# A shared ring of four PSUM buffers in a second layer's first spreading, and one-hots unpacked one and a half ranges ahead

## The chip, the cores and the metric

The kernel runs on one core of a Trainium2 chip. Times are device microseconds of that core. The engines are PE (TensorE: matmuls, with PEld for its weight loads), DVE (VectorE), ACT (ScalarE), POOL (GpSimd) and SP (SyncE, which here only issues DMAs). Each has its own instruction queue and works through it in order; they wait for each other by semaphores. Lines are those of the kernel before.

## The reference

Two layers of a graph network over 32,768 nodes of 128 features and 524,288 edges. The part that the change touches is the second layer: three rounds in which each node is mixed with a softmax memory and with the sum of its neighbours' scaled rows.

```python
# layer 0: x = layernorm(x + L0(x)); L0 sums x[src] into dst, has an MLP, attention and batch norms
for _ in range(3):                                   # layer 1
    q = x @ Wq.T + bq
    retrieved = softmax(q @ keys.T) @ values         # 512 keys
    deg = zeros(n).at[col].add(1.0);  dinv = rsqrt(deg)
    agg = zeros_like(x).at[row].add((dinv[:, None] * x)[col])      # over all edges
    lap = x - dinv[:, None] * agg
    x = 0.5 * x + 0.5 * (retrieved - 0.2 * lap)
x = layernorm(x_in + layernorm(x))
```

## The kernel before

Nodes are taken in 64 blocks (NB) of 512, a block in 4 chunks (NCH) of 128; a chunk of 128 nodes is also called a range, of which there are 256 (NW).

**Summing over edges** is done in two halves. *Spreading*: for each range of source nodes a one-hot matrix of 128 x 1536 (12 groups of 128 slots) copies the rows to slots of the outgoing edges. A row is 384 wide, three bf16 parts of an fp32 row of 128 (`split_steps`, L1394). `spread` (L1465) makes one *unit*: two matmuls (L1470, 128x128 by 128x384) into one `exp` tile of two PSUM banks, and one eviction of 128x768 into the bf16 tile `y_o`, by ACT (L1480) or by DVE (L1478). A range has KS = 6 units, a block 24. After every third unit half a range's slots, 576 KB, are stored by SP (L1483). `y_o` has two buffers, a range each. *Collecting*: `Sums` fetches for each range of targets the slots and some single rows (L1488, and POOL's indirect DMAs, L1497), builds one-hots (L1508) and adds with matmuls (L1522).

**The one-hot of a range** is kept in DRAM packed: its 1536 columns are three thirds, and each third has one bit of every packed byte. `ask_pick` calls `known_pick` (L1415), which has SP load the packed 64 KB (`three`, L1417). `unpack` calls `unpacked` (L1420), which takes them apart on DVE with one `bitwise_and` (`pick`, L1424). Before, `three` has three buffers and `pick` two (the pool's default).

**The second layer** is `layer1_grid` (L2042 on). It begins with a spreading by itself: the loop at L2298 over blocks, in pools `l1p`. It reads the first layer's result transposed (`v_d`), and so each block has a front part, `first`, that runs seven blocks ahead of the spreading: load `vT` and `x0`, `scale` on ACT (L2072), `turn` on PE (four transposes, L2077) with the addition to `x0` on DVE (L2078), `moments` on DVE (L2086, L2087), and for four blocks together a square root (L2092, L2093), then `norm` on DVE (L2098). `prepare` multiplies by dinv (L2109) and splits a row in three on ACT and DVE (L1403 to L1407). `emit` lists the 24 units and calls `ask_pick` two ranges ahead and `unpack` one range ahead, after the third unit of a range. Every third unit is DVE's. PSUM has eight banks: three `exp` tiles of two banks and two `tr` tiles of one for the transposes.

Then come two *steps* (pools `l1w`): collecting for state t, the softmax memory, and the spreading for state t + 1 woven together (every fourth unit is DVE's, two `exp` tiles), and a last step that collects only. `emit` is the same function in all of them.

The lists carry keys (`(12, turn)`), and `placed` sorts them into one program order. The spreading loop and the two steps are not in a `manual_schedule` block: a planner at build time orders the instructions of each engine's queue by its own costs, with the program order as the priority and the tiles' buffers as conditions.

Of the kernel before, what the change touches and what calls it, by code (L numbers as in the profile page):

```python
# [9 lines left out]
F32 = mybir.dt.float32  # L10
I32 = mybir.dt.int32
# [7 lines left out]
PSUM = bass.MemoryType.PSUM  # L19

P = 128
D = 128
BLK = 512
NCH = BLK // P
# [886 lines left out]
def tile_gnn_resnorm(ctx: ExitStack, tc: tile.TileContext, a: dict, out: bass.AP):  # L911
# [433 lines left out]
    def rows_of(t, i):  # L1345

        return t.rearrange("(b c p) d -> b p c d", c=NCH, p=P)[i]

    def kept_of(t, i):

        return t.rearrange("(b p c) d -> b p (c d)", c=NCH, p=P)[i]

    def flat(t):
        return t.rearrange("p c d -> p (c d)")
# [7 lines left out]
    class Exchange:  # L1362
# [50 lines left out]
            return t  # L1413

        def known_pick(self, wp, w):  # L1415
            packed = wp.tile([P, P], I32, name="three", bufs=3)
            nc.sync.dma_start(packed, pick_d[w])  # L1417
            return packed

        def unpacked(self, wp, packed):  # L1420


            pick = wp.tile([P, 3, P], I32, name="pick")
            nc.vector.tensor_tensor(pick, packed[:, None, :].to_broadcast([P, 3, P]),  # L1424
                                    gc["bits"].unsqueeze(2).to_broadcast([P, 3, P]), OP.bitwise_and)
            return pick.rearrange("p k n -> p (k n)").bitcast(FP8)
# [615 lines left out]
    def layer1_grid(v_d, s3, c3):  # L2042

        exs = [Exchange("src", slots_d[t % 2], rows_d[t]) for t in range(T_STEPS)]
        with tc.tile_pool(name="l1g", bufs=1) as gp:
# [3 lines left out]
            asked, picked = {}, {}  # L2049

            def ask_pick(wp, w):
                if w < NW:
                    asked[w] = exs[0].known_pick(wp, w)

            def unpack(wp, w):
                if w in asked:
                    picked[w] = exs[0].unpacked(wp, asked.pop(w))

            def first(b, st, wp, p_tr, group):

                k = b % NCH

                def load():
                    st["v"] = wp.tile([P, BLK], F32, name="vT", bufs=3)
                    nc.sync.dma_start(st["v"], v_d[b])
                    st["x0"] = wp.tile([P, NCH, D], F32, name="x1", bufs=2 * NCH)
                    nc.sync.dma_start(st["x0"], rows_of(a["x"], b))

                def scale():
                    nc.scalar.activation(st["v"], st["v"], AF.Identity, bias=c3, scale=s3)  # L2072

                def turn():
                    ps = p_tr.tile([P, NCH, P], F32, name="tr")
                    for c in range(NCH):
                        nc.tensor.transpose(ps[:, c, :], st["v"][:, c * P:(c + 1) * P], ident)  # L2077
                    nc.vector.tensor_add(st["x0"], st["x0"], ps)  # L2078

                def moments():  # L2080
                    if k == 0:
                        group["mv"] = wp.tile([P, NCH, NCH, 2], F32, name="ln_mvs")
                    st["mv"] = group["mv"]
                    t = wp.tile([P, NCH, 6], F32, name="ln_st")
                    for c in range(NCH):
                        nc.vector.bn_stats(t[:, c, :], st["x0"][:, c, :])  # L2086
                        nc.vector.bn_aggr(st["mv"][:, k, c, :], t[:, c, :])  # L2087
                    if k == 0:
                        group["rs"] = wp.tile([P, NCH, NCH], F32, name="ln_rss")
                    st["rs"] = group["rs"]  # L2090
                    if k == NCH - 1:
                        nc.scalar.activation(st["rs"], st["mv"][:, :, :, 1], AF.Sqrt, bias=eps_c)  # L2092
                        nc.vector.reciprocal(st["rs"], st["rs"])  # L2093

                def norm():
                    st["x"] = wp.tile([P, NCH, D], F32, name="xn", bufs=5)
                    for c in range(NCH):
                        nc.vector.tensor_scalar(st["x"][:, c, :], st["x0"][:, c, :], st["mv"][:, k, c, 0:1],  # L2098
                                                st["rs"][:, k, c:c + 1], op0=OP.subtract, op1=OP.mult)
                    nc.sync.dma_start(kept_of(xs_d[0], b), flat(st["x"]))  # L2100
                return load, [(7, scale), (12, turn), (15, moments)], [(14, norm)]

            def prepare(t, b, st, wp):
# [12 lines left out]
            def emit(t, b, st, wp, p_e, share):  # L2116

                ex = exs[t]
                y = {}

                def spread(n):
                    c, m = divmod(n, KS)
                    i = b * NCH + c
                    if m == 0:
                        ask_pick(wp, i + 2)
                        if i not in picked:
                            unpack(wp, i)
                    ex.spread(wp, p_e, "exp", i, picked[i], st["r"][:, c, :], m, y, n % share == share - 1,
                              WEIGHTS[m // 2])
                    if m == 2:  # L2130
                        unpack(wp, i + 1)
                    if m == KS - 1:
                        del picked[i]

                return [(n, lambda n=n: spread(n)) for n in range(NCH * KS)]
# [55 lines left out]
            def placed(*lists):  # L2191

                return [f for _, f in sorted((x for one in lists for x in one), key=lambda x: x[0])]
# [12 lines left out]
            def first_states(t, wp, p_s, p_tr):  # L2206

                for b in range(3):
                    ask_state(t, b, wp, p_s, p_tr)
                run(f for _, f in mems[0]["front"] + mems[0]["back"] + mems[1]["front"])  # L2210
# [77 lines left out]
            def run(steps):  # L2288
                for f in steps:
                    f()  # L2290

            with tc.tile_pool(name="l1p", bufs=2) as wp, \
                    tc.tile_pool(name="l1p_exp", bufs=3, space=PSUM) as p_e, \
                    tc.tile_pool(name="l1p_tr", bufs=2, space=PSUM) as p_tr:
                sts, firsts, norms, group = {}, {}, {}, {}
                for w0 in range(2):
                    ask_pick(wp, w0)
                for n in range(-NCH - 3, NB):  # L2298
                    b = n + NCH + 3
                    if b < NB:  # L2300
                        sts[b] = {}
                        load, firsts[b], norms[b] = first(b, sts[b], wp, p_tr, group)
                        load()
                    lists = []
                    if n + NCH + 2 in firsts:
                        lists.append(firsts.pop(n + NCH + 2))
                    if n + 2 in norms:
                        lists.append(norms.pop(n + 2))
                    if 0 <= n + 1 < NB:
                        lists.append(prepare(0, n + 1, sts[n + 1], wp))  # L2310
                    if n >= 0:
                        lists.append(emit(0, n, sts[n], wp, p_e, 3))
                    run(placed(*lists))
                    sts.pop(n, None)

            with tc.tile_pool(name="l1w", bufs=2) as wp, \
                    tc.tile_pool(name="l1_seg", bufs=2, space=PSUM) as p_g, \
                    tc.tile_pool(name="l1_exp", bufs=2, space=PSUM) as p_e, \
                    tc.tile_pool(name="l1_s", bufs=1, space=PSUM) as p_s, \
                    tc.tile_pool(name="l1_tr", bufs=1, space=PSUM) as p_tr:  # L2320
                for t in range(T_STEPS - 1):
                    sums = Sums(exs[t], wp, p_g, gc["iota1"], 2)
                    sts = {}
                    first_states(t, wp, p_s, p_tr)
                    for w0 in range(2):
                        ask_pick(wp, w0)
                    for n in range(-2, NB):
                        lists = []
                        if n + 1 in sts:
                            lists.append(prepare(t + 1, n + 1, sts[n + 1], wp))  # L2330
                        if n >= 0:
                            lists.append(emit(t + 1, n, sts[n], wp, p_e, 4))
                        b = n + 2
                        two_b = placed(*lists, *ahead(b))
                        if b < NB:
                            sts[b] = {}
                            weave(two_b, consume(t, b, sts[b], sums, wp, p_s, p_tr))
                        else:
                            run(two_b)
                        sts.pop(n, None)  # L2340
            with tc.tile_pool(name="l1z", bufs=2) as wp, \
# [6 lines left out]
                with tc.manual_schedule():  # L2348
# [3 lines left out]
                    for b in range(NB + 2):  # L2352
# [11 lines left out]
                        if b < NB:  # L2364
                            st = {}
# [95 lines left out]
```

## Time and profile before

Three runs: 14064.68, 14081.59 and 14114.55 us, median 14081.59. The profiled execution took 14078.42 us, its span from the first to the last instruction is 14076.6. Stages, by the starts and ends of their matmuls and loads, with the busy share of each engine in them (from the busy time of each stretch):

| stage | from, us | length, us | PE | DVE | ACT | POOL | clock | DMA share |
|---|---|---|---|---|---|---|---|---|
| sorting of edges, attention | 0 | 2345 | 85% | 80% | 48% | 37% | 0.93 | 0.06 |
| layer 0 spreading | 2345 | 1176 | 70% | 91% | 79% | 1% | 0.94 | 0.92 |
| layer 0 collecting, attention | 3521 | 2191 | 79% | 76% | 23% | 57% | 0.91 | 0.78 |
| layer 0 feed-forward | 5712 | 276 | 88% | 57% | 49% | 0% | 0.93 | 0.56 |
| layer 1 first spreading | 5988 | 1289 | 63% | 70% | 69% | 0% | 0.84 | 0.83 |
| layer 1 step 1 | 7277 | 2403 | 89% | 60% | 58% | 58% | 0.97 | 0.94 |
| layer 1 step 2 | 9680 | 2345 | 89% | 60% | 57% | 58% | 0.97 | 0.95 |
| layer 1 last step | 12025 | 2052 | 79% | 64% | 30% | 62% | 0.90 | 0.69 |

Over the whole span PE is busy 81%, DVE 70%, ACT 49%, POOL 44%, and the DMA engines move 251 GB/s. "Clock" is the TensorE clock that the throttle granted, 1.00 being full speed; "DMA share" is the mean busy share of the core's 16 DMA engines. A busy share is read together with what ends an engine's idle time: a stage in which no engine and no DMA stands near full is bound by their waiting for each other.

### The profile page before, as it was taken

The numbers are of one execution on the slowest core, as the hardware profiler recorded it, in microseconds if no ns is written. First come the engines' busy times: TensorE is split into PE (matmuls) and PEld (weight loads), VectorE is DVE, ScalarE is ACT, GpSimd is POOL, SyncE is SP. The second block draws the span as 40 slices with busy tenths as digits, with TensorE's granted clock in tenths as the row PEclk, the third lists the DMA queues.
The fourth block names the chain that finished last, engine by engine and source line by source line (L and its number), as shares of the span: only waits on it lengthen the run. The fifth ranks groups of instructions, "written<-read, shape, count | busy, mean of one in ns | idle before, by whom it ended". The sixth has DMA issues, their size and how long they took to land.

```text
span 14076.6 us, 165746 instructions
## 1 busy us (share of the span) xinstructions
PE 11459.8 (81%) x57832; PEld 5663.9 (40%) x57832; DVE 9833.9 (70%) x16418; ACT 6929.2 (49%) x10523; POOL 6149.7 (44%) x5525
## 2 busy tenths in 40 slices
PE   7898898777688888866668999897999888787887
PEld 2233233333333333322235555454555444344444
DVE  7978876997677777676656666565666555566667
ACT  4454455878122222466655665555665555333333
POOL 0273263000555555000015666554665555566665
PEclk9899998999899999988889999999999999898999
DMA  1000003999777877588879999998999999766676
GB/s 41 11 17 16 11 17 118 336 333 357 235 248 255 257 254 249 202 303 300 302 284 353 366 362 353 342 341 301 361 359 344 341 338 324 248 239 236 237 248 220
DMA packets 1401348, 3538.76 MB, mean 251 GB/s; under 512 B 218802, under 2 KB 633682, under 8 KB 1399346
## 3 DMA queue, kind: packets, MB, share of 16 engines
q1 hardware_dynamic: 960496, 2818.23, 55.1%
q0 software_dynamic: 252608, 520.41, 12.2%
q10 hardware_dynamic: 187394, 189.42, 4.1%
q8 instruction: 457, 7.49, 0.2%
q14 instruction: 393, 3.22, 0.1%
HBM read 2075.09 MB, written 1452.25 MB: 251 GB/s over the span
## 4 chain that ended last, share of the span: by engine, by line
PE 36%; DVE 8%; issue 5%; ACT 4%; another core or an unknown queue 3%; DMA 1%; SPq 0%; ACTq 0%; POOL 0%; DVEq 0%; POOLq 0%
PE seg L1522 14%; PE exp L1470 10%; PE s L2157 4%; PE s L2169 3%; DVE y_o L1478 3%; PE tr L2163 2%; ACT y_o L1480 2%; PE s L2149 1%; DVE oh L1508 1%; DMA slots<-y_o 1%; PE tr L2181 1%; PE tr L2143 1%; DVE pick L1424 0%; ACT pr L1064 0%
## 5 line engine op out<-in xcount | busy, mean ns | idle before, releaser
L1497 POOL DMA_INDIRECT listed<-rows,other x5120 | 5137.8, 1003 | 5234.2 <-issue 3027.3
L1470 PE MATMUL exp<-rows,pick 128*128 128x384 bf16 x10752 | 2620.3, 350 | 1004.0 <-ACT y_o L1480 309.6
L1480 ACT ACTIVATE y_o<-exp 128x768 bf16<-128x768 f32 x3328 | 2579.1, 811 | 1234.9 <-PE exp L1470 741.6
L1522 PEld LDWEIGHTS <-oh 128*128 128x128 bf16 x19456 | 1962.2, 101 | 2151.7 <-issue 1142.1
L1522 PE MATMUL seg<-y_i,oh 128*128 128x384 bf16 x12288 | 2586.9, 336 | 1.8 <-issue 1.5
L1470 PEld LDWEIGHTS <-pick 128*128 128x128 fp8e4 x10752 | 1082.2, 103 | 2355.1 <-issue 1552.1
L1478 DVE TENSOR_SCALAR y_o<-exp 128x768 bf16<-128x768 f32 x1280 | 1218.8, 952 | 832.8 <-PE exp L1470 559.8
L1688 ACT ACTIVATE pT<-s 128x1024 f32<-128x1024 f32 x1024 | 1047.8, 1024 | 1243.2 <-PE s L1663 822.9
L1522 PE MATMUL seg<-listed,oh 128*128 128x384 bf16 (+1 forms) x5120 | 1238.9, 341 | 356.6 <-ACT degs L2004 176.9
L1668 DVE TENSOR_REDUCE mx<-s 128x2 f32<-128x1024 f32 x1024 | 1244.7, 1219 | 314.7 <-PE s L1663 269.5
L1684 PE MATMUL s<-ql,k 32*128 32x512 f32 x4096 | 1222.1, 675 | 157.8 <-DVE mx L1668 145.1
L2233 DVE SCALAR_TENSOR_TENSOR part<-seg,dinv,part 128x128 f32<-128x128 f32 x1536 | 530.4, 345 | 1164.4 <-PE seg L1522 636.9
L1663 PE MATMUL s<-k,q 32*128 32x512 f32 x4096 | 1222.3, 677 | 15.8 <-ACT pT L1688 10.7
L1476 ACT CAST y_o<-exp 128x768 bf16<-128x768 f32 x1152 | 857.5, 809 | 241.8 <-PE exp L1470 172.1
L2157 PE MATMUL s<-keysT,qT 128*128 128x512 f32 x1536 | 830.3, 624 | 17.3 <-ACT qT L2151 6.3
L2163 PE MATMUL tr<-ident,pr 128*128 128x128 f32 x3072 | 536.4, 290 | 287.0 <-issue 216.7
L2169 PE MATMUL s<-pt,values 128*128 128x512 f32 x1536 | 722.5, 607 | 23.0 <-issue 20.1
L1508 DVE TENSOR_TENSOR oh<-iota,slot 128x2432 bf16<-128x2432 bf16 x512 | 724.6, 1415 | 7.5 <-PE tr L2163 4.2
L1062 DVE TENSOR_REDUCE nm<-s 128x1 f32<-128x512 f32 x768 | 517.8, 682 | 302.1 <-PE s L2157 106.8
L1508 DVE TENSOR_TENSOR oh<-ramp_p,slot 128x2432 bf16<-128x2432 bf16 x512 | 722.1, 1411 | 3.3 <-DMA slots<-y_o 3.2
L2164 ACT COPY pt<-tr 128x512 f32<-128x512 f32 x768 | 450.7, 588 | 469.6 <-remote 149.8
L1064 ACT ACTIVATE pr<-s,nm 128x512 f32<-128x512 f32 x768 | 528.8, 689 | 309.4 <-DVE nm L1062 187.5
(415 smaller groups left out, 15024.5 us busy)
## 6 DMA issues: line engine op xcount, KB each, us to landing
slots<-y_o SPq DMA_DIRECT2D x2048, 576.0 KB
y_i<-slots SPq DMA_DIRECT2D x1024, 1152.0 KB
listed<-rows,other POOLq DMA_INDIRECT x5120
rows<-rows SPq DMA_DIRECT2D x192, 384.0 KB
band<-row_dst SPq DMA_DIRECT2D x128, 384.0 KB
band<-row_src ACTq DMA_DIRECT2D x256, 192.0 KB
three<-pick SPq DMA_DIRECT2D x768, 64.0 KB
x_d<-xn SPq DMA_DIRECT2D x128, 256.0 KB
```

Of the source, the lines that this page charges most:

```text
L1470: nc.tensor.matmul(ps[:, j, :ROW], pick[:, o:o + P], r, start=True, stop=True)
L1478: nc.vector.tensor_scalar(dst, ps[:, :, :ROW], weight, None, op0=OP.mult)
L1480: nc.scalar.mul(dst, ps[:, :, :ROW], weight)
L1497: nc.gpsimd.indirect_dma_start(out=g[:, k, :], out_offset=None, in_=self.table, in_offset=bass.IndirectOffsetOnAxis(ap=index[:, k:k + 1], ...
L1508: nc.vector.tensor_tensor(oh.rearrange("p c (w z) -> p c w z", z=2), ramp.rearrange("p (w z) -> p w z", z=2)[:, None].to_broadcast([P, NC2 ...
L1522: nc.tensor.matmul(ps[:, :n], oh[:, j, :], src, start=(k == 0), stop=(k == NC2 - 1))
L1663: nc.tensor.matmul(ps[:, s % 2, :], t["q", o][32 * s:32 * s + 32, c * P:(c + 1) * P], t["k", o][32 * s:32 * s + 32, :], start=True, stop=True)
L1668: nc.vector.tensor_reduce(m[:, c, 2 * i:2 * i + 2, xr[o]], st[b].pop(("two", i)), AX.X, OP.max, negate=True)
L1684: nc.tensor.matmul(ps[:, s % 2, :], t["k", o][32 * s:32 * s + 32, c * P:(c + 1) * P], t["ql", o][32 * s:32 * s + 32, :], start=True, stop= ...
L1688: nc.scalar.activation(t["p", c][:, 2 * i:2 * i + 2, :], ps, AF.Exp)
L2157: nc.tensor.matmul(s, st["q"][:, c * P:(c + 1) * P], keysT, start=True, stop=True)
L2169: nc.tensor.matmul(ps, values[:, k, :], st["pt"][:, k, :], start=(k == 0), stop=(k == NCH - 1))
```

## The change

In the first spreading the `exp` ring goes from three tiles to four, which takes all eight banks; the transposes' own pool `p_tr` goes, and `turn` takes the first bank of an `exp` tile. In all spreadings of the second layer the one-hots are loaded three ranges ahead instead of two and unpacked at the fourth unit of a range (m == 3) for the range after the next, instead of at the third unit for the next; `three` gets four buffers and `pick` three.

```diff
         def known_pick(self, wp, w):
-            packed = wp.tile([P, P], I32, name="three", bufs=3)
+            packed = wp.tile([P, P], I32, name="three", bufs=4)
...
-            pick = wp.tile([P, 3, P], I32, name="pick")
+            pick = wp.tile([P, 3, P], I32, name="pick", bufs=3)
...
-            def first(b, st, wp, p_tr, group):
+            def first(b, st, wp, p_e, group):
...
                 def turn():
-                    ps = p_tr.tile([P, NCH, P], F32, name="tr")
+                    ps = p_e.tile([P, 2, BLK], F32, name="exp", tag="exp")[:, 0].rearrange("p (c n) -> p c n", c=NCH)
...
                     if m == 0:
-                        ask_pick(wp, i + 2)
-                        if i not in picked:
-                            unpack(wp, i)
+                        ask_pick(wp, i + 3)
+                        for k in (i, i + 1):
+                            if k not in picked:
+                                unpack(wp, k)
                     ex.spread(wp, p_e, "exp", i, picked[i], st["r"][:, c, :], m, y, n % share == share - 1,
                               WEIGHTS[m // 2])
-                    if m == 2:
-                        unpack(wp, i + 1)
+                    if m == 3:
+                        unpack(wp, i + 2)
...
-                    tc.tile_pool(name="l1p_exp", bufs=3, space=PSUM) as p_e, \
-                    tc.tile_pool(name="l1p_tr", bufs=2, space=PSUM) as p_tr:
+                    tc.tile_pool(name="l1p_exp", bufs=4, space=PSUM) as p_e:
...
-                for w0 in range(2):
+                for w0 in range(3):
                     ask_pick(wp, w0)
...
-                        load, firsts[b], norms[b] = first(b, sts[b], wp, p_tr, group)
+                        load, firsts[b], norms[b] = first(b, sts[b], wp, p_e, group)
...
                     first_states(t, wp, p_s, p_tr)
-                    for w0 in range(2):
+                    for w0 in range(3):
                         ask_pick(wp, w0)
```

## The prediction

> **What bounds the kernel now.** I read the stretches first (engine busy time, granted clock, DMA share and rate by time), then the waits of the stage that the change touches, then that stage in order of time. The second layer's first spreading runs from 5988 to 7277 us; two steps (7277 to 9680 and 9680 to 12025) hold the later spreadings. Three stretches of 200 us, from the first spreading, a later step and the last step (us; then busy us and instruction count of PE, PEld, DVE, ACT, POOL; clock, DMA share, GB/s):
>
> ```profile
> 6600.00:6800.00 200.00, 124.92 (x514) 59.35 (x515) 137.34 (x272) 136.71 (x190) 0.00 (x0) 0.84 0.82 302
> 7800.00:8000.00 200.00, 184.75 (x979) 106.00 (x978) 129.84 (x216) 123.68 (x206) 121.36 (x119) 1.00 0.99 371
> 13000.00:13200.00 200.00, 155.73 (x722) 87.44 (x721) 125.02 (x315) 59.46 (x109) 121.13 (x126) 0.89 0.68 230
> ```
>
> In the first spreading nothing is full: PE 62%, DVE 69%, ACT 68%, DMA 0.82. It is bound by engines waiting for each other. In the later step PE stands at 92% and the DMA engines at 0.99: there a removed wait of DVE or ACT buys little.
>
> The timeline repeats: the run of 12 matmuls at 6612.90 has its like at 7104.40, 24 blocks later, so a block takes 491.5 / 24 = 20.48 us. Over that window DVE is busy 338.72 us (14.1 a block), ACT 335.77 (14.0), PE 306.75 (12.8). Its longest waits (who <- whom: us, times, longest):
>
> ```profile
> ACT y_o L1480 <- PE exp L1470: 109.9, 147, 1.2
> PE exp L1470 <- DVE y_o L1478: 85.5, 90, 1.3
> DVE y_o L1478 <- PE exp L1470: 70.5, 85, 1.5
> DVE x L2078 <- PE tr L2077: 63.6, 24, 3.1
> PE exp L1470 <- ACT y_o L1480: 60.7, 84, 2.0
> ```
>
> PE waits for a ring buffer that DVE or ACT still reads (85.5 + 60.7 us, 6.1 a block), and then both wait for PE to refill it (DVE 2.9, ACT 4.6). This is a ring that is one buffer short whenever DVE turns to other work. DVE's 14.1 busy and 6.4 idle make the 20.48; 2.9 of the idle are for exp and 63.6 / 24 = 2.65 for the transposes. Why the transposes are late stands in DVE's and PE's queues (start, length; idle before in brackets):
>
> ```profile
> 6618.87 0.55 DVE L1424 TENSOR_TENSOR pick<-three,lane 128x384 int32<-128x384 int32 x1
> 6622.47 0.69 DVE L2078 TENSOR_TENSOR x<-x,tr 128x512 f32<-128x512 f32 x1 [3.05 <-PE tr L2077]
> ```
>
> ```profile
> 6617.15 0.81 PE L1470 MATMUL exp<-rows,pick 128*128 128x384 bf16 x4 [0.72 <-DVE y_o L1478]
> 6619.48 2.10 PE L1470 MATMUL exp<-rows,pick 128*128 128x384 bf16 x6 [1.52 <-DVE pick L1424]
> 6621.37 1.06 PE L2077 MATMUL tr<-ident,vT 128*128 128x128 f32 x4
> ```
>
> At 6617.96 PE is done with a range, and the next one's one-hot is still in DVE's queue behind an eviction. PE idles 1.52 us, then does six matmuls and the transposes, and DVE stands 3.05 us before x. This happens once a block.
>
> **What the stage does without the transposes.** The block look-ahead ends seven blocks early, and the last blocks have no scale, transposes, addition or moments. PE's runs after the same wait then come one block apart (48 matmuls):
>
> ```profile
> 7201.41 1.14 PE L1470 MATMUL exp<-rows,pick 128*128 128x384 bf16 x6 [1.12 <-DVE y_o L1478]
> ...
> 7217.29 3.58 PE L1470 MATMUL exp<-rows,pick 128*128 128x384 bf16 x12 [1.12 <-DVE y_o L1478]
> ...
> 7233.18 3.60 PE L1470 MATMUL exp<-rows,pick 128*128 128x384 bf16 x12 [0.40 <-DVE y_o L1478]
> ```
>
> A block takes 15.9 us there with the old ring, though only 2.4 us of DVE work (x 0.69, moments 4 x (0.27 + 0.17)) and 0.8 of ACT's are gone. So of 4.6 us that the rest costs each block, at least half is waiting.
>
> **The change, part by part.**
> (1) One-hots earlier. L1424 is issued as often as before (256 in the stage, 0.55 us each), one range sooner, and its third buffer lets it run while two ranges are held. The 1.52 us of PE idle go, and DVE's wait for the transposes falls by the same: **-1.5 us a block** as long as PE has a buffer to go on with. Its load moves a range earlier in SP's queue: 256 issues of 0.42 us as before, one more at each stage's start, ahead of slot stores that wait for evictions anyway (SP <- DVE y_o: 743 us over the stage). Nothing for it.
> (2) Ring of four. With three buffers kept in turn, a unit holds one for 3 x 20.48 / 24 = 2.56 us. Four at the same hold, with the transposes as a 25th unit, give 25 x 2.56 / 4 = 16.0 us a block. Holds grow if units queue at ACT or DVE, whose busy 14.1 and 14.0 are the floor below. Between 16.0 and 20.48 - 1.5 = 19.0 the engines alone should land near 16.5.
> (3) Transposes in the ring. Before, they had two buffers of their own and waited for none; no row shows their wait for a shared one. Nearest are PE's waits for exp buffers: 0.25 us in the steady runs, 1.13 after a long DVE stretch. So 14 to 64 us over 57 blocks. No gain is possible from sharing itself. I take the lower, inside the 16.5, because a fourth buffer is free more often.
> (4) What is late next: **the stores**. A block moves 8 slot stores of 576 KB, rows 384, four one-hot loads of 64 and three transfers of 256: 6,016 KB = 6.16 MB, which at 20.48 us is the 301 GB/s of the trace. At 16.5 us it would need 373. The later steps hold 341 and 342 GB/s over their whole length (share 0.94 and 0.95) and 371 in their best 200 us (0.99). And the y_o tile has two buffers: a range's stores must land before the next range but one is evicted. In the tail at 15.9 us a block the first such wait of size appears (PE 2.86 us at 7264, put down to ACT). So DMA sets the block: 6.16 MB / 352 GB/s (the rate of a 2000 us stretch in the first of the later steps) = **17.5 us**, with bounds 6.16 / 371 = 16.6 and 6.16 / 338 = 18.2 (338 is the layer 0 spreading's mean).
> The Trainium skill (DMA: Bandwidth & Descriptors, Specifications) gives about 358 GB/s as one core's HBM limit; by it a block would take 17.2 us and the sum would be 17 us lower. The 371 of the trace lies above it, so here the measurement decides.
> The skill also describes PE pausing briefly at each turn of its PSUM buffers until its clock swings between half and full (TensorE: Matmul & The Clock Gate, "A second HAM failure mode"). The trace agrees, 0.84 granted in this stage against 1.00 in the later step, and 12 matmuls in 3.53 us where six took 1.15; by that rule fewer pauses shorten PE too, which the DMA bound would hide.
> (5) Later spreadings. Ring and engines stay; only L1424 and its load move. PE's wait for the one-hot is 16.4 us in both steps together and DVE's wait for the load 67.3, on an engine that is 60% busy. I take **-15 us**. The queues are not in program order here (a planner outside the hand-ordered parts sorts them), so other rows may shift: the two steps run the same code and differ by 2403 - 2345 = 58 us, which I keep as the bound either way.
>
> **The sum.** 57 blocks (6010 to 7173) x (20.48 - 17.5) = 170; the seven last are at 15.9, where 5.5 MB need as much at 347 GB/s: 0. Profiled execution 14078.4 (span 14076.6): 14078.4 - 170 - 15 = 13,893. Its time is 3 us under the median of the runs, less than the step of my estimates, so **13,895 us**. Its own range, by 16.6 and 18.2 us a block and +-58 for the later steps taken at half weight: 13,810 to 13,965.
>
> **Rivals.**
> *A. DMA keeps up.* Rates up to 371 are there; against it, they last 200 us and y_o has two buffers. 57 x 3.9 = 222, less 15 more: 13,840.
> *B. The ring buys nothing, the one-hot does.* DVE works in order: while it stands at moments and norm, the fourth buffer holds a unit for DVE itself (every third unit), and ACT still starves. For it: 85.5 us of PE's waits are for DVE. Against it: the refill that DVE waits for (2.9 a block) is just what the spare unit covers. 57 x 1.2 to 1.5: about 14,005.
> *C. Slower: the transposes block the ring.* In PE's queue they may stand ahead of the next units while vT is still behind ACT's evictions, or keep a buffer until DVE, behind an eviction and a one-hot (0.95 + 0.55), adds x. Then PE pays what only DVE pays now, up to 3.05 us a block, against 1.5 saved: 57 x 1.5 = +86, 14,165. It decides from the point at which a block's new wait exceeds 1.5 us plus what the fourth buffer gives. Against it: vT is scaled at 6618.38, 3 us before its transposes.
> *D. It does not do what it says.* The planner puts the one-hots back behind the evictions, or trades the gain for another order: 14,060 to 14,090.
>
> **Chances.** Forecast 0.52, A 0.17, B 0.17, C 0.08, D 0.06. A measurement of this kernel tells about 0.3%, 42 us, from no change. Faster: forecast, A and most of B (0.13) make 0.82; same: the rest of B and D, 0.10; slower: 0.08. The range reaches from A's lower part (16.6 and a good later step) to B: 13,800 to 14,030.
>
> **What would show it.** Right: in the first spreading no PE wait for L1424, DVE's wait for transposes under half of 140 us, blocks 17 to 18 us apart, DMA share at 0.93 or more at some 345 to 355 GB/s, waits of ACT or DVE y_o for slot stores growing from 8 us to tens, clock above 0.84; the next step starting some 170 us earlier. Wrong: blocks at 19 us with DMA at 0.88 (B); PE waits ahead of L2077 and no shorter stage (C); a first spreading shortened while the two later steps give back more than 60 us.

## The result and the profile after

The changed kernel takes 13919.08 us (median of 4 runs, 13878.98 to 13953.84) against 14098.07 for the kernel before (4 runs with the one taken beside it, 14064.68 to 14147.31): a ratio of 0.9854, 95% interval 0.9826 to 0.9882. 13,895 was forecast. The profiled execution took 13916.68 us, its span is 13914.9.

Where the 161.7 us between the two spans lie, with the first spreading taken from its first packed one-hot load to the first fetch of slots, the steps from there to the last slot store, the last step from there to the end:

| us | all before it | first spreading | two steps | last step | span |
|---|---|---|---|---|---|
| before | 5987.8 | 1293.1 | 4745.3 | 2050.4 | 14076.6 |
| after | 5985.5 | 1101.8 | 4724.8 | 2102.8 | 13914.9 |
| difference | -2.3 | -191.3 | -20.5 | +52.4 | -161.7 |

Two stretches of the changed kernel, from the first spreading and from a later step (us; busy us and count of PE, PEld, DVE, ACT, POOL; clock, DMA share, GB/s):

```profile
6600.00:6800.00 200.00, 134.24 (x610) 66.16 (x609) 166.25 (x327) 158.82 (x226) 0.00 (x0) 0.88 0.98 362
7800.00:8000.00 200.00, 183.80 (x946) 103.68 (x945) 125.20 (x212) 123.55 (x205) 127.35 (x121) 0.98 0.99 360
```

In the first spreading DVE has gone from 137 busy us to 166, ACT from 137 to 159, and the DMA engines from share 0.82 to 0.98 and from 302 GB/s to 362. The later step looks much as it did. The waits of the whole first spreading (who <- whom: us, times, longest), before:

```profile
ACT y_o L1480 <- PE exp L1470: 257.8, 370, 1.2
PE exp L1470 <- DVE y_o L1478: 213.9, 239, 1.4
...
PE exp L1470 <- ACT y_o L1480: 164.6, 234, 2.9
DVE x L2078 <- PE tr L2077: 144.8, 57, 3.1
...
PE exp L1470 <- DVE pick L1424: 80.6, 54, 1.5
...
ACT y_o L1480 <- DMA slots<-y_o: 5.8, 8, 3.0
```

and after:

```profile
PE exp L1470 <- DVE y_o L1478: 194.4, 343, 1.4
PE exp L1470 <- ACT y_o L1480: 139.2, 115, 2.6
DVE y_o L1478 <- PE exp L1470: 118.6, 203, 1.1
...
ACT y_o L1480 <- PE exp L1470: 67.2, 116, 1.5
...
ACT y_o L1480 <- DMA slots<-y_o: 28.4, 42, 2.2
...
DVE x L2078 <- PE exp L2077: 4.9, 4, 2.7
...
DVE y_o L1478 <- DMA slots<-y_o: 2.6, 2, 2.1
```

DVE's wait for the transposes fell from 144.8 us over the stage to 4.9, PE's for the one-hot from 80.6 to none, and the waits of ACT and DVE for slot stores rose from 8.4 to 31.0. PE's waits for a ring buffer went from 378 us to 334, in a shorter stage as large a share as before (29% and 30%), but they no longer starve ACT: its wait for PE is 67 us, where it was 258. PE's queue (start, length; idle before):

```profile
6607.85 2.34 PE L1470 MATMUL exp<-rows,pick 128*128 128x384 bf16 x12 [1.12 <-DVE y_o L1478]
6610.36 0.48 PE L1470 MATMUL exp<-rows,pick 128*128 128x384 bf16 x2 [0.17 <-DVE y_o L1478]
6610.69 0.60 PE L2077 MATMUL exp<-ident,vT 128*128 128x128 f32 x4
...
6624.73 2.34 PE L1470 MATMUL exp<-rows,pick 128*128 128x384 bf16 x12 [1.13 <-DVE y_o L1478]
```

The same run of 12 returns after 16.88 us, a block; it was 20.48. Over the 53 blocks from the third to the 55th the mean is 17.1 us, and 20.3 before. The transposes follow the unit before them without a pause.

### The profile page after: what moved, and what is told of

Its sections match the earlier page's. It is cut to its first block, busy times and chain, and to the rows that moved or that the text cites. A ratio compares the mean times of both kernels' runs of the same rounds, so it can differ in the third digit from the quotient of the medians.

```text
span 13914.9 us, 165702 instructions
## 1 busy us (share of the span) xinstructions
PE 11388.9 (82%) x57832; PEld 5651.0 (41%) x57832; DVE 9841.0 (71%) x16418; ACT 6905.2 (50%) x10523; POOL 6158.1 (44%) x5525
## 5 line engine op out<-in xcount | busy, mean ns | idle before, releaser
L1470 PE MATMUL exp<-rows,pick 128*128 128x384 bf16 x10752 | 2552.3, 342 | 872.0 <-ACT y_o L1480 310.8
L1480 ACT ACTIVATE y_o<-exp 128x768 bf16<-128x768 f32 x3328 | 2550.5, 813 | 1037.4 <-PE exp L1470 546.1
L2158 PE MATMUL s<-keysT,qT 128*128 128x512 f32 x1536 | 829.5, 623 | 29.8 <-issue 17.1
L1508 DVE TENSOR_TENSOR oh<-iota,slot 128x2432 bf16<-128x2432 bf16 x512 | 724.9, 1416 | 6.1 <-PE seg L1522 3.1
L1508 DVE TENSOR_TENSOR oh<-ramp_p,slot 128x2432 bf16<-128x2432 bf16 x512 | 722.4, 1411 | 3.7 <-DMA slots<-y_o 3.6
```

The costliest lines, as they stand in the source:

```text
L1470: nc.tensor.matmul(ps[:, j, :ROW], pick[:, o:o + P], r, start=True, stop=True)
L1480: nc.scalar.mul(dst, ps[:, :, :ROW], weight)
L1508: nc.vector.tensor_tensor(oh.rearrange("p c (w z) -> p c w z", z=2), ramp.rearrange("p (w z) -> p w z", z=2)[:, None].to_broadcast([P, NC2 ...
L2158: nc.tensor.matmul(s, st["q"][:, c * P:(c + 1) * P], keysT, start=True, stop=True)
```

## The experiments

No edit changes what is computed; two of them add loads that nothing reads. Runs of one group share a chip, and absolute times differ between chips by up to 10% (see the end), so ratios are to the kernel before on the same chip, and the stage lengths come from each run's profile. The first spreading of the unedited kernel before is 1293.1 us on two chips, that of the changed kernel 1101.8 and 1101.3.

| edit | first spreading, us | two steps | last step | ratio to before, 95% interval |
|---|---|---|---|---|
| *group 1* changed kernel again | 1101.3 | 4272.9 | 1700.5 | 0.9867 (0.9850 to 0.9883) |
| one-hots alone | 1245.8 | 4288.7 | 1704.2 | 0.9970 (0.9958 to 0.9983) |
| shared ring of four alone | 1107.4 | 4266.5 | 1696.3 | 0.9853 (0.9837 to 0.9870) |
| one-hots, shared ring of three | 1211.4 | 4280.5 | 1697.9 | 0.9946 (0.9929 to 0.9962) |
| *group 2* kernel before again | 1293.1 | 4270.3 | 1698.5 | one run |
| changed, three y_o buffers | 1038.3 | 4272.1 | 1696.8 | 0.9806 (0.9789 to 0.9822) |
| changed, two more loads a block | 1162.9 | 4277.9 | 1697.4 | one run |
| before, two more loads a block | 1280.5 | 4268.9 | 1695.8 | one run |
| *group 3* three y_o, one-hots a range earlier still | 1006.6 | 4711.8 | 2063.4 | 0.9727 (0.9698 to 0.9755) |
| ring of four alone, three y_o | 1311.3 | 4779.6 | 2078.2 | 0.9988 (0.9972 to 1.0005) |
| changed, four y_o | 1309.4 | 4703.8 | 2084.7 | 0.9976 (0.9949 to 1.0002) |
| four y_o, one-hots a range earlier still | 1075.9 | 4720.9 | 2061.5 | 0.9813 (0.9783 to 0.9842) |

**The changed kernel and the kernel before again.** No edit.

> The changed kernel once more, nothing edited. In its first profile the first spreading (first packed one-hot load to first fetch of slots) fell from 1293 to 1102 us, the two steps from 4745 to 4725, and the last step, whose code is untouched, rose from 2050 to 2103. If the rise is the scatter of a stage that the change does not reach, the last step lies anywhere from 2030 to 2110 here while the first spreading stays within 3 us of 1102. If the change lengthens the last step, it is at 2095 to 2110 again.

> The kernel before, nothing edited, on the chip of this group: first spreading 1290 to 1296 us. Two steps: as long as with the changed one-hots to within 20 us if these bring nothing in the steps, 20 us or more longer if they do. Last step: as long as in the other kernels of the group to within 20 us if the 52 us between the first two profiles were scatter.

The first spreading repeats to a microsecond. On these two chips the steps take 4272.9 with the changed one-hots and 4270.3 with the old: nothing is gained there. The last step is 1700.5 and 1698.5, and in the four kernels of group 3, on a chip with times like those of the first pair, it lies between 2061.5 and 2084.7, with old and new one-hots alike: most of the 52 us between the first two profiles was scatter.

**The parts, one at a time.** One-hots alone:

```diff
-                    tc.tile_pool(name="l1p_exp", bufs=4, space=PSUM) as p_e:
+                    tc.tile_pool(name="l1p_exp", bufs=3, space=PSUM) as p_e, \
+                    tc.tile_pool(name="l1p_tr", bufs=2, space=PSUM) as p_tr:
```

with `first` given `p_tr` and `turn` a tile of it again, all against the changed kernel.

> One-hots ahead alone, in all spreadings; ring of three and the transposes' own two buffers as before. My theory (each part frees its own wait, the stores bind only when both are there): the 1.5 us a block that PE waits for the one-hot go and little else, first spreading 1293 - 57 x 1.5 = about 1208 us. Rival 'the one-hots do it all': 1102. Rival 'the ring does it all': 1285 to 1293. Later steps: 4725 if the one-hots bring what the changed kernel showed there, 4745 if that was scatter.

Measured 1245.8: 47 us, not 85. The two waits that were to go did go or nearly so (PE waits for no one-hot, DVE 34.8 us for the transposes, where it was 144.8), but PE then stands somewhere else. PE's queue with the one-hots alone:

```profile
6005.41 0.60 PE L2077 MATMUL tr<-ident,vT 128*128 128x128 f32 x4
6006.01 0.48 PE L1470 MATMUL exp<-rows,pick 128*128 128x384 bf16 x2
6008.69 3.64 PE L1470 MATMUL exp<-rows,pick 128*128 128x384 bf16 x11 [2.19 <-DVE y_o L1478]
```

PE reaches the transposes without a wait, and a unit later the three buffers are full: 2.19 us behind DVE, which works at x and moments before its next eviction. The wait moved by one stretch of DVE work.

Ring of four alone: the lines of the diff in `first` and its call, `turn` and the pools, with the one-hots as before.

> Ring of four shared with the transposes alone; one-hots as before. My theory: the refill waits go, the one-hot wait of 1.5 us a block stays: 16.5 + 1.5 = 18.0 us a block, first spreading 1293 - 57 x 2.5 = about 1150 us, with PE still waiting some 80 us for the one-hot. Rival 'the one-hots do it all': 1285 to 1293. Rival 'the ring does it all': 1102. Later steps: 4745.

Measured 1107.4, the whole gain but 6 us. The one-hots still come late; waits of its first spreading:

```profile
PEld L1470 <- DVE pick L1424: 139.0, 246, 1.3
PE exp L1470 <- DVE pick L1424: 51.6, 50, 1.1
...
ACT y_o L1480 <- DMA slots<-y_o: 15.7, 21, 3.0
```

PE waits 51.6 us for them and it costs next to nothing: with a filled spare buffer ACT and DVE work through that wait (ACT waits 55 us for PE in this stage and DVE 127; with the changed one-hots too it is 67 and 119).

One-hots with a ring of three that the transposes share (`bufs=3` in the changed kernel).

> The changed kernel with a ring of three, still shared with the transposes (two PSUM banks stay unused): the sharing without the fourth buffer. My theory: the sharing costs 0.25 to 1.1 us a block, 14 to 64 us over 57 blocks, against the one-hots alone: first spreading 1220 to 1275 us. Rival 'sharing blocks the ring' (the slower one of the prediction): over 1293.

Measured 1211.4, below the expected band and 34 us below the one-hots with the transposes' own buffers. Sharing did not cost here. The two differ in the queues' order too, since the planner sorts them anew; which of it made the 34 us was not tried.

**Is it the DMA rate?** Three y_o buffers (`exs[0].kept = 3` ahead of the loop), and, in both kernels, two more loads of `v_d[b]` per block into a tile with four buffers that nothing reads:

```diff
                     nc.sync.dma_start(st["x0"], rows_of(a["x"], b))
+                    for _ in range(2):
+                        more = wp.tile([P, BLK], F32, name="more", bufs=4)
+                        nc.sync.dma_start(more, v_d[b])
```

> The changed kernel with three y_o buffers instead of two in the first spreading. My theory (the DMA engines are full at share 0.97 and some 362 GB/s, so their rate binds): the waits of ACT and DVE for slot stores, some 30 us there, turn into other waits, first spreading 1085 to 1102 us. Rival (the depth of y_o binds, not the rate): those 30 us go and the stage falls to 1070 or less, with GB/s above 370.

> The changed kernel with two more loads of a block of v_d (2 x 256 KB a block) into a tile that nothing reads; the outputs are as before. My theory (DMA rate binds): 64 x 0.524 MB / 362 GB/s = 93 us more, first spreading about 1190 us at an unchanged rate. Rival (the engines bind at 17 us a block): 1102 to 1115, at a rate of some 390 GB/s.

> The kernel before with the same two extra loads a block. Its DMA engines have room there (share 0.82, 301 GB/s), so both theories expect 0 to 15 us more than the 1293 of the first spreading and a rate of about 327 GB/s; a rise of over 50 us would mean that the loads cost something else than DMA rate, and e5_after_mb would not tell the theories apart.

Stretches of 800 us in the first spreadings (columns as above) of the changed kernel with three y_o buffers, of the changed kernel with the loads, and of the kernel before with the loads:

```profile
5820.00:6620.00 800.00, 559.21 (x2608) 263.80 (x2607) 692.39 (x1363) 668.65 (x964) 0.00 (x0) 0.92 1.01 384
```

```profile
5820.00:6620.00 800.00, 530.91 (x2309) 261.23 (x2308) 635.99 (x1259) 601.34 (x854) 0.00 (x0) 0.85 0.99 371
```

```profile
5820.00:6620.00 800.00, 505.47 (x2090) 233.74 (x2090) 582.29 (x1138) 564.28 (x776) 0.00 (x0) 0.84 0.92 337
```

A third y_o buffer took the stage to 1038 us at 384 GB/s, and the waits for slot stores from 31.0 us to 6.6, so the 362 GB/s of the changed kernel was no ceiling: a busy share of 0.97 still had 6% to give. The loads cost the changed kernel 61.6 us, where an unchanged rate makes 93 and free engines 0 to 14; the kernel before became 12.6 us faster with them, which neither theory expected and which was not followed up. So the changed kernel does stand at its transfers, but at how soon the stores of two buffers land, and not at a rate. The 63 us that the third buffer brought are more than the waits for stores that went; which other waits make up the rest was not taken apart.

**What binds next.** The one-hots a range earlier (`ask_pick(wp, i + 4)`, `unpack(wp, i + 3)`, `pick` four and `three` five buffers) and the depth of y_o (`exs[0].kept`).

> Three y_o buffers, and one-hots one range earlier still (loaded four ahead, unpacked for three ahead at the fourth unit, pick with four buffers and three with five). With three y_o buffers the first spreading took 1038 us at 384 GB/s and DMA share 1.01, and PE waited 103 us for one-hots. Theory 1 (with three buffers the DMA rate binds at last): 1025 to 1045 us whatever the one-hots do, the one-hot wait becomes another. Theory 2 (the late one-hot binds again): some 100 us less than 1038, at over 400 GB/s.

> Shared ring of four with three y_o buffers, one-hots as in the kernel before. Theory 1 (the one-hots matter only where the ring is short): 1035 to 1050 us, as with the changed one-hots. Theory 2 (the ring alone reached 1107 us only because the stores' two buffers hid the late one-hot): with the stores out of the way the one-hot wait shows, 1070 us or more.

> The changed kernel with four y_o buffers in the first spreading. If the depth of y_o has stopped binding at three (4.5 us of waits for slot stores were left there): 1030 to 1042 us. If it still binds: 1010 or less, at over 390 GB/s.

> Four y_o buffers and one-hots a range earlier: the two last edits together. If the DMA rate binds at three buffers: 1020 to 1042 us, and no more than 10 us from e8_yo3_early and e10_yo4. If two waits hid each other: 1000 or less.

All four surprised. Three y_o buffers with the earlier one-hots took 1006.6 us at 397 GB/s, 18 below the band of theory 1 and far above the second's. The ring alone with three y_o buffers fell to theory 2, which had set no upper end, but lost all that the ring had brought (1311.3). Four y_o buffers missed both theories, alone (1309.4) and with the earlier one-hots (1075.9). The stretch of 800 us of the first and the waits for stores in it:

```profile
6200.00:7000.00 800.00, 546.67 (x2668) 269.55 (x2666) 708.03 (x1389) 685.52 (x987) 0.00 (x0) 0.96 1.03 397
```

```profile
ACT y_o L1480 <- DMA slots<-y_o: 46.0, 57, 2.3
...
DVE y_o L1478 <- DMA slots<-y_o: 12.9, 23, 2.1
```

With that many transfers the waits for stores are back, 59 us in 800, in spite of the third buffer. Waits and queues of the changed kernel with four y_o buffers:

```profile
PE exp L1470 <- DVE pick L1424: 299.7, 155, 3.2
DVE y_o L1478 <- PE exp L1470: 248.0, 283, 2.2
```

```profile
6603.31 0.55 DVE L1424 TENSOR_TENSOR pick<-three,lane 128x384 int32<-128x384 int32 x1
```

```profile
6603.91 3.58 PE L1470 MATMUL exp<-rows,pick 128*128 128x384 bf16 x12 [3.05 <-DVE pick L1424]
```

PE waits for a one-hot once a range (155 times in 800 us of about 5.1 us a range), and uses it 50 ns after it is there. How far ahead a one-hot stands can be counted in DVE's queue: DVE evicts the third and the last unit of every range, and the trace shows how many of these evictions stand ahead of a range's L1424. In ranges, counted over the ranges 24 to 219:

| | in program order | in DVE's queue | there, for one range in four | first spreading, us |
|---|---|---|---|---|
| before | 0.5 | 0.5 | 0 | 1293.1 |
| ring of four alone | 0.5 | 0.5 | 0 | 1107.4 |
| changed | 1.5 | 1.5 | 1 | 1101.8 |
| changed, three y_o | 1.5 | 0.5 | 0 | 1038.3 |
| three y_o, one-hots a range earlier | 2.5 | 1.5 | 1 | 1006.6 |
| ring of four alone, three y_o | 0.5 | 0 | 0 | 1311.3 |
| changed, four y_o | 1.5 | 0 | 0 | 1309.4 |
| four y_o, one-hots a range earlier | 2.5 | 0.5 (13 times 1) | 0 | 1075.9 |

With two y_o buffers the planner keeps the program's order but for one range in four. With more it puts L1424 back by half a range to two, behind evictions and norm. Where that leaves it behind both evictions of the range before, in every range, PE waits some 464 us for one-hots over the stage and the ring brings nothing; half a range ahead in three ranges of four, PE waits 52 to 103 us and the ring of four brings most of its gain. Two pairs that differ in the one-hots' edit alone show it: 1311.3 and 1038.3 with three y_o buffers, 1309.4 and 1075.9 with four. And where the one-hots stand alike, the third y_o buffer brings 69 us (1107.4 to 1038.3) or 95 (1101.8 to 1006.6). Why the planner moves them was not tried, nor a hand-written order. The fastest version of the study is three y_o buffers with the earlier one-hots: 13759.02 us against 14128.9 on its chip.

## Why the prediction was right, and where its steps were not

**Right.** The stage, the sign and the size: 170 us were forecast for the first spreading and 191.3 came, 185 in all and 161.7 (spans) or 179 (medians). That the total is so near is partly luck: the first spreading brought 21 us more than forecast, and in the profiled pair the last step, which was not to move, took 52 back. What was to be seen is there: blocks of 17.1 us (17 to 18 forecast), DMA share 0.97 (at 360 GB/s, where 345 to 355 had been named), no wait for L1424, the transposes' wait a thirtieth, waits for stores grown from 8.4 to 31.0, clock from 0.84 to 0.89, the next step 194 us earlier. On the clock, the Trainium skill (TensorE: Matmul & The Clock Gate, "A second HAM failure mode") describes PE pausing at the turn of its PSUM banks so often that the clock swings between half and full. The rows do not show that rule at work: PE waited at the ring 473 times in 1293 us before and 458 times in 1102 us after, no more seldom, and the clock rose all the same.

**Step 1, the one-hots (1.5 us a block): mis-sized.** Alone they bring 47 us, 0.8 a block, and beside the ring 6. The step set the condition that PE has a buffer to go on with; with three it has not.

**Step 2, the ring: right mechanism, mis-sized.** The engines were to reach 19.0 with the one-hots alone and 16.5 with both. The ring alone does 186 of 191 us. The count of buffers, each held 2.56 us a unit, gave 16.0 a block and was the better guide than adding waits up: with three y_o buffers the stage runs at 1038 us, 16.1 a block. The last seven blocks, put at no gain, went from 16.4 us to 15.3.

**Step 3, sharing: no cost seen.** 14 to 64 us were the bounds of its cost; with a ring of three, sharing went with 34 us less. That sharing itself gains is not shown, since the queues' order differs too.

**Step 4, DMA sets the block: right place, wrong kind of bound.** 17.5 us came from a rate of 352 GB/s that other stages hold (their best 200 us hold 373, not 371); the stage held 362, and up to 397 with other buffers. What binds is the landing of a range's stores with two y_o buffers, which the step named beside the rate and did not price, so it is luck that 17.5 is near the measured 17.1; rival A (DMA keeps up, 16.6 us a block) missed that by as little. The Trainium skill (DMA: Bandwidth & Descriptors, Specifications) gives about 358 GB/s as one core's limit, a stack's 716 divided by two cores. Over 800 us the changed kernel held 362, and 384 and 397 with three y_o buffers; the measurement decides, and 358 is no ceiling for this kernel on one core.

**Step 5, later spreadings (-15 us): open.** On one chip the old one-hots take 4266.5 and the changed ones 4272.9 to 4288.7, on another 4268.9 and 4270.3 against 4272.1 and 4277.9: there they bring nothing. On the chips with the longer times it is the other way round in every profile: 4745.3 before against 4724.8 in the first pair, 4779.6 with the old one-hots against 4703.8 to 4720.9 with earlier ones in group 3. Two kernels of group 3 with first spreadings alike (1311.3 and 1309.4) differ by 49 us in their medians of ten runs, the one with the changed one-hots being shorter. So the -20.5 of the first pair need not be scatter; what makes the difference between chips was not tried.

**Rivals.** B (the ring buys nothing) is the reverse of what happened. C did not occur. D did not occur in the changed kernel, whose queue keeps the one-hots 1.5 ranges ahead, and 1 once a block; it did occur with four y_o buffers, and took the whole gain.

## What to carry to other kernels

Where one engine serves a ring in order and also does other work, count buffers by how long a unit holds one; a spare buffer hides inputs that are late now and then, so the two gains do not add, but not inputs that are late every time. A DMA share near 1 does not prove a rate limit: add a staging buffer and see whether GB/s rise. Where a planner orders the queues, read the lead from the trace and not from the source, and look again after every change of a buffer count: from three to four y_o buffers the first spreading went from 1038 us to 1309.

## What was not expected of the hardware

The same kernel before takes 12873.5 and 12874.2 us on the chips of groups 1 and 2, and 14098 and 14129 beside the first pair and in group 3 (fast and slow chips, below). The first spreading is 1293.1 us on both kinds; the time before it (5988 and 5618 us), the steps and the last step, in all of which POOL gathers, differ. Two stretches of the last step, on a slow and on a fast chip:

```profile
12400.00:12600.00 200.00, 157.86 (x739) 88.08 (x737) 126.20 (x318) 60.49 (x112) 124.15 (x129) 0.90 0.68 232
```

```profile
11400.00:11600.00 200.00, 178.84 (x888) 101.39 (x887) 158.32 (x400) 72.86 (x134) 152.43 (x157) 0.98 0.85 286
```

Single instructions are as long (a gather 968 and 966 ns, the one-hot L1508 1414 and 1415), but in the six profiles on slow chips the trace puts waits of 1403 to 1563 us in all, single ones up to 35 us, down to another core or an unknown queue, and on the fast ones none. What they are stays open.
